# A batch of two attentions on one core: the third item's denominators, the projection's additions and the last weight sums

## The chip, the cores and the metric

The kernel runs on one core of a Trainium2 chip. The metric is the time of one launch on the device, in microseconds; the median of several runs is given, and one more execution was recorded by the hardware profiler.

## The reference

For each of 16 images (256 channels, 32 x 32 = 1024 positions) two layers are computed, all in float32. The part that matters here is the second attention, with 8 heads of 32 channels:

```python
# layer 0: 4 heads of 64 channels
qkv = (xs @ w_proj + b_proj).reshape(B, S, N_HEADS, 3 * D_K)
attn = softmax(einsum('bihd,bjhd->bijh', q, k) * SCALE, axis=2)
x = einsum('bijh,bjhd->bihd', attn, v) @ w_out + b_out + xs
# layer 1: 8 heads of 32 channels, then an MLP
x = x + attention(group_norm(x, gn1_w, gn1_b), qkv_w, proj_w, proj_b, phys_bias)
h = group_norm(x, gn2_w, gn2_b)
return x + mlp_w2 @ gelu(mlp_w1 @ h + mlp_b1) + mlp_b2
```

## The kernel before

One image of the batch is called b here. For each b the kernel runs attention a (layer 0), attention b (layer 1) and the MLP, and it weaves the pieces of the neighbouring images into them: while attention b of image b runs, TensorE also makes the MLP's output for image b - 1 (tiles m, lines 1180 and on) and q, k, v of layer 0 for image b + 1 (tiles v_a). A stage is a Python generator; after each of its steps, functions that were put off with `later.after(steps, fn)` and have come due are run, and the pieces of other work for that step are issued. So the order of the instructions on an engine is mostly the order in which this Python runs.

Attention b (`attention_b`) works through four items: (t, c) with t one of two halves of 512 positions, and c one of two groups of four heads. An item takes eight blocks of 128 keys in four steps of two blocks. In a step, `scores` makes the scores s_b on TensorE (line 569) and their exp e_b on ScalarE (line 582), `weigh` multiplies the exps of the step before with v (acc_b, line 619), and `add` sums the exps over the key blocks on VectorE into the tile es_b (line 595), which becomes the softmax's denominator. Results of single steps are copied out by ScalarE (lines 630 and 634) and added by VectorE (line 603); the very last one of a stage is added from PSUM (line 637).

For images 1 to 14 (`by_fold`) the denominators of the first three items, i = 0 to 2, go through `fold`: two DMAs, one on SP's queue and an accumulating one on GpSimd's, pack the sums into a tile packed_b (lines 649 and 650). A few steps later `normalise_folded` makes the denominators with 16 small matmuls (den_b, line 659). The fourth item, i = 3, goes through `normalise`, with 8 matmuls from es_b itself (den_b, line 676). Both call `denominators`: ScalarE copies the row out of PSUM (line 376), a DMA on SP spreads it over the partitions (sp_b, line 381), VectorE takes the reciprocal (line 387), DMAs on SP write it to a row in DRAM (lines 391 or 398) and read it back onto all partitions (rd_b, line 403), and `scale` multiplies the item's result with it (line 701). GpSimd keeps two running totals (lines 399 and 400).

When both items of a half t are scaled, `out_proj` multiplies with the projection's weights (tiles j, line 357). For t = 0 of images 1 to 14 there is a spare place, the other half of the tile packed_b: ScalarE copies the product with its bias there (line 745), VectorE adds it to x (line 748) and takes statistics for the coming group norm (line 753). The projection of t = 1 is handed to attention a of the next image and is issued at that stage's thirteenth step.

PSUM has two single banks (0 and 1, `bank`) and three pairs (`wide`). acc_b uses bank 0, den_b bank 1. The exps stand in a ring of four tiles (`weights_tile`); an exp of attention b takes a whole tile per key block, one of attention a half a tile. `tc.keep_in_program_order(ins)` holds an instruction where it was issued; `with tc.issue_after(ins)` puts what is issued in it behind ins on that engine.

Of the kernel before, what the change touches and what calls it, by code (L numbers as in the profile page):

```python
# [259 lines left out]
def first_pass(ctx, tc, x, out, k):  # L260
    nc = tc.nc
# [3 lines left out]
    later = Later()  # L265
# [44 lines left out]
    def wide(name, n=None):  # L310
        if n is None:
            n = next(m for m in order if m not in kept)
        use(n)
        return ps_s.tile([P, 2, TB], F32, tag=f"s{n}", name=name)

    def bank(name, n):
        return ps_a.tile([P, TB], F32, tag=f"b{n}", name=name)
# [36 lines left out]
    def product(o, w, r, **flags):  # L354
        for c0 in range(0, P, cols[0]):
            sl = slice(c0, c0 + cols[0])
            nc.tensor.matmul(o[sl], w[:, sl], r, **flags)  # L357
# [15 lines left out]
    spread_out, spare = {}, {}  # L373

    def denominators(key, den, d, full, waits, then, parts=1):
        nc.scalar.copy(d, den)
        n = full.shape[1]
        w = 4 * TB // P
        spread = work.tile([P, w], F32, tag="spread", name=f"sp_{key}", bufs=2)
        row = dram.tile([4 * TB // n, n], F32, tag="row", name=f"row_{key}", bufs=4)  # L380
        nc.sync.dma_start(
            spread, d[:: 32 // parts].rearrange("p (a b) -> p a b", b=w)
        )

        def invert():
            inverse = work.tile([P, w], F32, tag="inverse", name=f"inv_{key}", bufs=2)
            tc.keep_in_program_order(nc.vector.reciprocal(inverse, spread))
            if parts > 1:
                num = P // parts
                for r in range(parts):  # L390
                    nc.sync.dma_start(
                        row[:, r * n // parts : (r + 1) * n // parts].rearrange(
                            "g (a b) -> g a b", b=w
                        ),
                        inverse[r * num : (r + 1) * num],
                    )
            else:
                nc.sync.dma_start(row.rearrange("r (a b) -> (r a) b", b=w), inverse)
            nc.gpsimd.tensor_add(dsum, dsum, spread)  # L399
            nc.gpsimd.tensor_add(isum, isum, inverse)  # L400
            num = P * n // (4 * TB)
            for r in range(P // num):
                spread_out["last"] = nc.sync.dma_start(
                    full[r * num : (r + 1) * num], row[r].partition_broadcast(num)
                )
            later.after(waits[1], lambda: then(full))

        later.after(waits[0], invert)
# [133 lines left out]
    def attention_b(b, qT, kT, v, project):  # L542
        key, D = f"b_{b}", D1
        G = P // D


        by_fold = 0 < b < B - 1
# [3 lines left out]
        units = [(i, kb) for i in range(len(items)) for kb in range(0, SB, 2)]  # L551
# [36 lines left out]
        def add(i, kb, es):  # L588
            if kb == 0:
                sums[i] = work.tile([P, G, TB], F32, tag="es", name=f"es_{key}_{i}", bufs=2)  # L590
            step = G if by_fold else G // 2
            for m in range(kb == 0, 2):
                for g in range(0, G, step):
                    d = sums[i][:, g : g + step]
                    ins = nc.vector.tensor_add(  # L595
                        d, (d if kb else es[0][:, g : g + step]), es[m][:, g : g + step]
                    )
                    if by_fold or m or g:
                        tc.keep_in_program_order(ins)
                    yield  # L600
            while parts:
                r, part = parts.pop(0)
                tc.keep_in_program_order(nc.vector.tensor_add(r, r, part))
# [41 lines left out]
        def fold(i, r):  # L645
            if i == 0:
                packs.append(act.tile([P, 4, TB], F32, tag="res", name=f"packed_{key}"))
            packed = packs[0][:, i % 2 * 2 : i % 2 * 2 + 2]
            nc.sync.dma_start(packed, sums[i][:HALF])
            nc.gpsimd.dma_start(packed, sums[i][HALF:], accum_op=ALU.add)  # L650
            later.after(3 if i else 4, lambda: normalise_folded(i, r, packed))

        def normalise_folded(i, r, packed):
            c = items[i][1]
            q = TB // G
            den = bank(f"den_{key}_{i}", 1)[:, :q]
            for m in range(2):
                for n in range(G):
                    nc.tensor.matmul(
                        den[n * D : (n + 1) * D, :], k["folded"][:, c, m],  # L660
                        packed[:, m, n * q : (n + 1) * q], start=m == 0, stop=m == 1,
                    )
            if i == 1:
                spare["home"] = packs[0]
            full = work.tile([P, TB], F32, tag="full", name=f"rd_{key}_{i}", bufs=2)
            denominators(
                f"{key}_{i}", den, full[:, :q], full, (1, 2 if i < 2 else 4),
                lambda full: scale(i, r, False, full), G,
            )
# [29 lines left out]
        def scale(i, r, last, full):  # L699
            t, c = items[i]  # L700
            tc.keep_in_program_order(nc.vector.tensor_mul(r, r, full))
            if c == CC - 1:
                issue = project(t, res[t])
                if last and b + 1 < B:
                    handed.append(issue)
                else:
                    later.after(1, issue)
# [3 lines left out]
        for u in units:  # L711
            now = scores(*u)
            adds = add(*now)
            if pending:
                if not by_fold and now[1]:
                    next(adds)
                weigh(*pending)
            else:
                yield
            for _ in adds:  # L720
                pass
            if pending:
                yield
            pending = now
# [6 lines left out]
    def out_proj(key, w, src, bias, xs, t, stats, then):  # L731
        todo = list(range(CC))

        def issue(cos=range(CC), apart=False):
            home = None if apart else spare.pop("home", None)
            apart = apart or cols[0] == P
            if not apart:
                both = wide(f"{key}_{t}")
            ps = {}

            def leave(co):
                y = xs[:, co, t * TB : (t + 1) * TB]
                if home is not None:
                    held = home[:, 2 + co]
                    nc.scalar.activation(
                        held, ps[co], AF.Identity, bias=bias[:, co : co + 1]
                    )
                    nc.vector.tensor_add(y, y, held)
                else:
                    nc.vector.scalar_tensor_tensor(  # L750
                        y, ps[co], bias[:, co : co + 1], y, ALU.add, ALU.add
                    )
                nc.vector.bn_stats(stats[:, co, t, :], y)
                todo.remove(co)

            for co in cos:
                ps[co] = bank(f"{key}_{t}_{co}", co) if apart else both[:, co, :]
                for kc in range(CC):
                    product(
                        ps[co],  # L760
                        w[:, kc, co * P : (co + 1) * P],
                        src(kc),
                        start=(kc == 0),
                        stop=(kc == CC - 1),
                    )
                if apart:
                    leave(co)
            if not apart:
                for co in cos:
                    leave(co)  # L770
            if not todo and then:
                then()

        return issue
# [945 lines left out]
```

## Time and profile before

| | |
|---|---|
| median of 3 runs | 3627.85 us (3626.86 to 3628.85) |
| the profiled execution's own time | 3625.52 us |
| its span, from the first to the last instruction | 3623.4 us |
| TensorE clock granted, mean | 0.999 |
| VectorE: es_b, 128x2048 (line 595, adding to the sum) | 336 times, mean 2287 ns |
| VectorE: es_b, 128x1024 (line 595, images 0 and 15) | 96 times, mean 1218 ns |
| VectorE: x plus packed_b (line 748) | 28 times, mean 678 ns |
| VectorE: statistics (line 753) | 128 times, mean 687 ns |
| TensorE: den_b from packed_b (line 659) | 672 times in 42 groups of 16 |

The distance from the first line 748 of one image to that of the next is 223 to 224 us. Tile names are printed without their numbers, so den_b stands for the denominators of every image and item, and the line tells the kind. A group of matmuls that run side by side in parts of the array has a busy time that is shorter than the sum of its durations; where times within TensorE are compared, the start of one group is subtracted from the start of the next.

### The profile page before, as it was taken

The numbers are of one execution on the slowest core, as the hardware profiler recorded it, in microseconds if no ns is written. First come the engines' busy times: TensorE is split into PE (matmuls) and PEld (weight loads), VectorE is DVE, ScalarE is ACT, GpSimd is POOL, SyncE is SP. The second block draws the span as 40 slices with busy tenths as digits, with TensorE's granted clock in tenths as the row PEclk, the third lists the DMA queues.
The fourth block names the chain that finished last, engine by engine and source line by source line (L and its number), as shares of the span: only waits on it lengthen the run. The fifth ranks groups of instructions, "written<-read, shape, count | busy, mean of one in ns | idle before, by whom it ended". The sixth has DMA issues, their size and how long they took to land.

```text
span 3623.4 us, 81637 instructions
## 1 busy us (share of the span) xinstructions
PE 3590.2 (99%) x35565; PEld 1470.2 (41%) x35565; DVE 2775.8 (77%) x3153; ACT 2283.5 (63%) x3197; POOL 244.0 (7%) x317
## 2 busy tenths in 40 slices
PE   9999999999999999999999999999999999999998
PEld 3434344343443434434344443444434444343433
DVE  5586887768778687876868778688786977868887
ACT  4665757657575675756658566585765757657572
POOL 4000100001000010000100001010010100000000
PEclk9999999999999999999999999999999999999999
DMA  3011321213122131221312213121121212213100
GB/s 129 10 50 37 59 78 34 77 33 71 60 40 72 39 81 45 49 67 34 81 45 52 66 33 81 45 55 63 42 73 44 55 62 48 72 39 65 59 22 23
DMA packets 81571, 198.29 MB, mean 55 GB/s; under 512 B 37974, under 2 KB 38742, under 8 KB 75062
## 3 DMA queue, kind: packets, MB, share of 16 engines
q1 hardware_dynamic: 71828, 164.39, 14.9%
q0 software_dynamic: 7632, 28.21, 5.1%
q8 instruction: 280, 4.59, 0.5%
q10 hardware_dynamic: 1746, 0.40, 0.1%
q14 instruction: 85, 0.70, 0.1%
HBM read 125.85 MB, written 22.27 MB: 41 GB/s over the span
## 4 chain that ended last, share of the span: by engine, by line
PE 77%; DVE 12%; issue 4%; DMA 4%; SPq 2%; ACT 1%; DVEq 0%; ACTq 0%; POOL 0%; POOLq 0%
PE s_a L428 12%; PE acc_a L451 12%; PE m L1097 10%; PE s_b L569 8%; PE m L357 7%; DVE es_b L595 7%; PE acc_b L619 7%; PE qk_b L1003 3%; PE qk_a L1003 3%; PE v_b L357 3%; PE o L357 3%; PE j L357 2%; DMA rd_b<-row_b 2%; PE qk7y_b L1003 1%; PE qk7y_a L1003 1%
## 5 line engine op out<-in xcount | busy, mean ns | idle before, releaser
L582 ACT ACTIVATE e_b<-s_b 128x1024 f32<-128x1024 f32 (+1 forms) x1280 | 982.1, 865 | 137.0 <-PE s_b L569 137.0
L595 DVE TENSOR_TENSOR es_b<-es_b,e_b 128x2048 f32<-128x2048 f32 (+1 forms) x432 | 880.6, 2049 | 103.8 <-ACT e_b L582 86.0
L438 ACT ACTIVATE e_a<-s_a 128x1024 f32<-128x1024 f32 x512 | 520.6, 1024 | 360.4 <-PE s_a L428 356.2
L428 PE MATMUL s_a<-q,k 64*64 64x512 f32 x4096 | 544.4, 593 | 0.0
L451 PE MATMUL acc_a<-e_a,v 64*64 64x512 f32 x4096 | 540.3, 589 | 0.0
L569 PE MATMUL s_b<-q,k 32*64 32x512 f32 x8192 | 527.4, 600 | 4.0 <-DVE res_b L637 2.0
L465 DVE TENSOR_TENSOR es_a<-es_a,e_a 128x1024 f32<-128x1024 f32 x384 | 473.5, 1233 | 59.5 <-ACT e_a L438 36.2
L619 PE MATMUL acc_b<-e_b,v 128*32 128x512 f32 x4096 | 492.1, 598 | 0.0
L357 PE MATMUL m<-g,w 128*32 128x256 f32 (+1 forms) x6456 | 416.6, 385 | 0.0
L357 PEld LDWEIGHTS m<-g,w 128*32 128x32 f32 x6456 | 223.9, 111 | 204.3 <-issue 58.9
L451 PEld LDWEIGHTS acc_a<-e_a,v 64*64 64x64 f32 x4096 | 188.2, 133 | 251.3 <-issue 214.9
L569 PEld LDWEIGHTS s_b<-q,k 32*64 32x64 f32 x8192 | 175.8, 130 | 257.5 <-issue 132.6
L428 PEld LDWEIGHTS s_a<-q,k 64*64 64x64 f32 x4096 | 176.1, 133 | 246.5 <-issue 209.1
L619 PEld LDWEIGHTS acc_b<-e_b,v 128*32 128x32 f32 x4096 | 108.5, 109 | 351.6 <-ACT e_b L582 194.7
L1097 PE MATMUL m<-gn_h,w 128*128 128x512 f32 x512 | 242.5, 602 | 2.9 <-DVE x L1222 1.3
L595 DVE TENSOR_TENSOR es_b<-e_b,e_b 128x2048 f32<-128x2048 f32 (+1 forms) x72 | 147.0, 2050 | 127.6 <-ACT e_b L582 127.6
L1161 DVE TENSOR_TENSOR g<-g,g 128x512 f32<-128x512 f32 (+1 forms) x185 | 195.5, 1068 | 1.2 <-PE m L357 0.8
L1097 PE MATMUL m<-hs,w 128*128 128x512 f32 x384 | 177.9, 592 | 0.1
L1112 ACT ACTIVATE g<-g,m1b 128x512 f32<-128x512 f32 x128 | 91.5, 720 | 110.9 <-DVE g L1141 83.4
L1097 PEld LDWEIGHTS m<-gn_h,w 128*128 128x128 f32 x512 | 93.1, 190 | 118.8 <-issue 101.1
L1112 ACT ACTIVATE g<-m,m1b 128x512 f32<-128x512 f32 x128 | 80.9, 683 | 76.7 <-PE m L1097 76.7
L399 POOL TENSOR_TENSOR dsum<-dsum,sp_b 128x16 f32<-128x16 f32 x63 | 72.9, 1157 | 795.8 <-DMA sp_b<-rd_b 795.8
(214 smaller groups left out, 3591.9 us busy)
## 6 DMA issues: line engine op xcount, KB each, us to landing
w<-w_kept SPq DMA_DIRECT2D x30, 1792.0 KB
packed_b<-es_b SPq DMA_DIRECT2D x42, 512.0 KB
packed_b<-es_b POOLq DMA_DIRECT2D x42, 512.0 KB, 6.2
d_a<-row_a SPq DMA_DIRECT2D x64, 256.0 KB
rd_b<-row_b SPq DMA_DIRECT2D x252, 64.0 KB
out_dram<-x SPq DMA_DIRECT2D x63, 256.0 KB
x<-in_x_dram SPq DMA_DIRECT2D x30, 512.0 KB
qk<-qk_kept SPq DMA_DIRECT2D x14, 1024.0 KB
```

Of the source, the lines that this page charges most:

```text
L357: nc.tensor.matmul(o[sl], w[:, sl], r, **flags)
L428: nc.tensor.matmul(s[h : h + HALF, g, :], kT[g * D : (g + 1) * D, c, kb * P + h : kb * P + h + HALF], qT[g * D : (g + 1) * D, c, t * TB : ...
L438: nc.scalar.activation(e, s, AF.Exp, scale=float(D) ** -0.5)
L451: nc.tensor.matmul(accs[i][h][g * D : (g + 1) * D, :], v[h * HALF : (h + 1) * HALF, kb, c * 2 + g], e[h * HALF : (h + 1) * HALF, g, :], st ...
L465: nc.vector.tensor_add(sums[i], held[i] if kb == 1 else sums[i], e)
L569: nc.tensor.matmul(outs[g][h : h + HALF, :], kT[g * D : (g + 1) * D, c, k0 : k0 + HALF], qT[g * D : (g + 1) * D, c, t * TB : (t + 1) * TB] ...
L582: nc.scalar.activation(to, s, AF.Exp, scale=float(D) ** -0.5)
L595: ins = nc.vector.tensor_add(d, (d if kb else es[0][:, g : g + step]), es[m][:, g : g + step])
L619: nc.tensor.matmul(acc[g * D : (g + 1) * D, :], v[:, kb + m, c * G + g], es[m][:, g, :], start=(m == 0), stop=(m == 1),)
L1003: nc.tensor.matmul(to, w, x[right], start=first, stop=True, skip_group_check=not first)
L1097: nc.tensor.matmul(ps, blocks[1][number - 1][:, i * P : (i + 1) * P], inputs[b][number], start=first, stop=True, skip_group_check=not first,)
L1161: (nc.vector.tensor_add if plus else nc.vector.tensor_sub)(d, d, more)
```

## The change

There are four edits. The denominators of the third item (i = 2) are made four steps after its fold instead of three. In the last step of the fourth item the weight sums are taken in halves of 1024 columns instead of whole tiles of 2048. The additions of the projection of t = 0 to x and their statistics are put off by one step, and they are placed behind the last weight sum on VectorE. To have that place, every weight sum of attention b is remembered in `spread_out["es"]`.

```diff
@@ -588,13 +588,15 @@
         def add(i, kb, es):
             if kb == 0:
                 sums[i] = work.tile([P, G, TB], F32, tag="es", name=f"es_{key}_{i}", bufs=2)
-            step = G if by_fold else G // 2
+            step = G if by_fold and (i, kb) != units[-1] else G // 2
             for m in range(kb == 0, 2):
                 for g in range(0, G, step):
                     d = sums[i][:, g : g + step]
                     ins = nc.vector.tensor_add(
                         d, (d if kb else es[0][:, g : g + step]), es[m][:, g : g + step]
                     )
+                    spread_out["es"] = ins
+                    spread_out["es"] = ins
                     if by_fold or m or g:
                         tc.keep_in_program_order(ins)
                     yield
@@ -648,7 +650,7 @@
-            later.after(3 if i else 4, lambda: normalise_folded(i, r, packed))
+            later.after(3 if i == 1 else 4, lambda: normalise_folded(i, r, packed))
@@ -745,13 +747,19 @@
                     nc.scalar.activation(
                         held, ps[co], AF.Identity, bias=bias[:, co : co + 1]
                     )
-                    nc.vector.tensor_add(y, y, held)
+                    later.after(1, lambda: add_up(co, y, held))
+                    return
                 else:
                     nc.vector.scalar_tensor_tensor(
                         y, ps[co], bias[:, co : co + 1], y, ALU.add, ALU.add
                     )
                 nc.vector.bn_stats(stats[:, co, t, :], y)
                 todo.remove(co)
+
+            def add_up(co, y, held):
+                with tc.issue_after(spread_out["es"].ins):
+                    nc.vector.tensor_add(y, y, held)
+                    nc.vector.bn_stats(stats[:, co, t, :], y)
```

The two programs have the same instructions on every engine except VectorE, which has 28 more (two per image 1 to 14). At the end of attention b of each of these images VectorE's order becomes: four sums of 1024 columns, the addition to x, line 603's addition, the statistics, the second addition and its statistics, line 637's addition, the third item's reciprocal, the fourth item's reciprocal, two sums of attention a (line 465), and then the scaling of the third item (line 701). Before, it was: two additions to x, two statistics, two sums of 2048 columns, line 603, the third reciprocal, line 637, the scaling of the third item, the fourth reciprocal, and then the sums of attention a. On TensorE the 16 matmuls of the third item's denominators move from ahead of the projection j to behind the acc_b of the following step, ahead of a v_a; on ScalarE their copy moves accordingly. On SP the fourth item's spread (line 381) moves ahead of the four reads (line 403) of the third item's rows.

## The prediction

> **What bounds the kernel now.** I read the page first (who is busy, the chain that ended last), then the waits, then the order of time at the one place that the change touches, on TensorE and on VectorE. The page and its chain:
>
> ```profile
> span 3623.4 us, 81637 instructions
> PE 3590.2 (99%) x35565; PEld 1470.2 (41%) x35565; DVE 2775.8 (77%) x3153; ACT 2283.5 (63%) x3197; POOL 244.0 (7%) x317
> PE 77%; DVE 12%; issue 4%; DMA 4%; SPq 2%; ACT 1%; DVEq 0%; ACTq 0%; POOL 0%; POOLq 0%
> ```
>
> TensorE is busy 99% of the span, so work moved on VectorE counts only where TensorE waits for it. The edit acts in items 1 to 14 of the batch, at the end of the second attention. In the table of waits the largest VectorE wait there is not TensorE's:
>
> ```profile
> DVE room_b L701 <- DMA rd_b<-row_b: 96.6, 15, 7.7
> ```
>
> That is VectorE idle for 6.4 us per item before the third item's scaling (L701), behind which the next attention's sums stand. The order of time of TensorE, for item 4, shows that TensorE runs on through it (start, length, what; in brackets the idle time before it):
>
> ```profile
> 1096.05 0.62 PE L659 MATMUL den_b<-packed_b,folded 128*32 128x128 f32 x16
> 1096.49 3.62 PE L357 MATMUL j<-res_b,wpj 128*32 128x512 f32 x32
> 1100.04 2.54 PE L569 MATMUL s_b<-q,k 32*64 32x512 f32 x32
> 1102.51 1.92 PE L619 MATMUL acc_b<-e_b,v 128*32 128x512 f32 x16
> 1104.25 1.91 PE L357 MATMUL v_a<-wp,x 128*32 128x256 f32 x32
> 1105.98 1.90 PE L619 MATMUL acc_b<-e_b,v 128*32 128x512 f32 x16
> 1107.69 1.91 PE L357 MATMUL v_a<-wp,x 128*32 128x256 f32 x32
> 1110.13 1.07 PE L676 MATMUL den_b<-es_b,eones 128*32 128x512 f32 x8 [0.53 <-DVE es_b L595]
> ```
>
> The only gap is at the fourth item's denominators (L676), which need the last weight sums. By start times it is longer: the last v_a takes 1110.13 - 1107.69 = 2.44 us until the next start, the one before it 1.73, so 0.71 us are lost. VectorE's order shows why the sums are late:
>
> ```profile
> 1096.58 0.69 DVE L701 TENSOR_TENSOR res_b<-res_b,rd_b 128x512 f32<-128x512 f32 x1 [1.81 <-DMA rd_b<-row_b]
> 1097.18 0.68 DVE L1226 TENSOR_TENSOR x<-x,packed_b 128x512 f32<-128x512 f32 x1
> 1097.79 4.68 DVE L595 TENSOR_TENSOR es_b<-es_b,e_b 128x2048 f32<-128x2048 f32 x2
> 1102.38 0.71 DVE L603 TENSOR_TENSOR room_b<-room_b 128x512 f32<-128x512 f32 x1
> 1103.02 1.28 DVE L748 TENSOR_TENSOR x<-x,packed_b 128x512 f32<-128x512 f32 x2
> 1104.22 1.27 DVE L753 BATCH_NORM_STATS2 st<-x 128x6 f32<-128x512 f32 x2
> 1105.42 4.66 DVE L595 TENSOR_TENSOR es_b<-es_b,e_b 128x2048 f32<-128x2048 f32 x2
> 1109.99 0.69 DVE L603 TENSOR_TENSOR room_b<-room_b 128x512 f32<-128x512 f32 x1
> ```
>
> From L701 on VectorE does not idle until the last sum ends near 1110.06. L701 itself (second item's scaling) waits for a DMA, and the projection j needs its result too. So both engines start from one event, the end of L701 at 1097.27, and race to L676: VectorE gets there after 1110.13 - 1097.27 = 12.86 us, TensorE would be earlier.
>
> **What the Trainium skill says.** "VectorE: DVE Perf Modes", section "Side-by-side: where the cycles go for N=2048 bf16", counts one result a cycle in the 1x mode plus some 158 cycles at 0.96 GHz; I estimate 2298 ns for 2048 columns and 1231 for 1024. The trace agrees: the two forms of L595 have means of 2287 and 1218 ns. "PSUM — Partial Sum Buffer", section "Engine vs sequencer instructions", calls the queues of ScalarE and VectorE strict FIFO and TensorE's matmuls in program order; so an instruction is late with whatever stands ahead of it, as the chain above shows. "DMA: Bandwidth & Descriptors", section "Latency and other measured facts", gives a DMA about 2 us of fixed cost; here the small transfer of a denominator (L381, issued at 1098.35) ended GpSimd's wait at 1100.34, 2.0 us.
>
> **The change part by part.** Times are relative to the first L748 of an item (1103.02 in item 4), read from the order of time of all fourteen items; L701 of the second item ends at -5.75 in each.
>
> *Denominators a step later.* The 16 matmuls of L659 go from ahead of j to behind the acc_b that starts at 1102.51, ahead of a v_a. From start to start they take 0.43 or 0.44 us in all 42 groups of the trace, 28 of them between an acc_b and 256-column matmuls as in the new place: I take 0.44, bounds 0.4 and 0.7. In front of j nothing is won unless L701 was not the limit. The later part of j cannot start before -5.69 (item 1: 427.95, its L748 at 433.64). In nine items (1, 4, 5, 8, 9, 10, 13, and 3 and 7 within 0.05) j already ends at -2.98 to -2.93, set by L701; in 2, 6, 12 it is 0.04 to 0.09 later, in 11 and 14 it is 0.46 and 0.53 later. Afterwards all end at about -2.98. The waits of L659 for its packing DMA (0.15 to 1.01 us before j in items 3, 6, 7, 8, 9, 12) go, but j then waits for L701 instead.
>
> *Additions behind the last sums.* Two L748 and two L753 stood in front of the sums: 1105.42 - 1103.02 = 2.40 us. Moved behind, the sums start at 0.0 instead of 2.40. Nothing reads these columns of x before the group norm, which comes after the other half's j, 29 us later (462.58 in item 1). What is queued behind them is L637, which frees bank 0 for acc_a; see below.
>
> *1024 columns.* Four adds for two: 4 x 1.16 us from start to start (four in a row take 4.63 in the first item) against 4.66: nothing. Each half follows its own exp; the last exp ends at +2.13, before the fourth half starts at 3.48. The sums end at 4.7 instead of 7.06.
>
> *The sum for TensorE.* From j's end at -2.98: s_b 2.47 (part of it a wait for ScalarE's copy of j, L745, which stays), acc_b 1.74, L659 0.44, v_a 1.73, acc_b 1.72, v_a 1.73. L676 starts at +6.85, and what is late next is TensorE itself, the sums being there 2.1 us earlier. Before, L676 started at +7.12 in 13 items and +7.47 in item 12. Saved: 13 x 0.27 + 0.62 = 4.1 us. With L659 at its bounds of 0.4 and 0.7 the gain is 4.7 to 0.5.
>
> *The rest of VectorE.* After the sums: add, L603, statistics, add, statistics, L637, each 0.6 from start to start: L637 ends near 8.35, before 8.46; acc_a needs its bank at 10.7. The third reciprocal comes at 8.25 instead of 7.58, and its four row writes on SP follow. SP now issues the fourth item's spread (L381) ahead of the four reads of the third's rows, at about 11.1 instead of 13.4, so the fourth reciprocal runs at about 13.1; the third's L701 now stands behind it and two of the next sums (L465). VectorE still stands still, parked at that reciprocal from 8.5 to 13.1, but L465 starts near 13.3 instead of 15.96. The rows land about 0.7 + 0.6 later, at 16.4, when L701 comes up: little wait. L465 was not holding TensorE at 15.96 (no gaps in the next 10 us), so starting earlier is worth nothing. The loads of w and x behind these issues start about 1 us earlier, also worth nothing. ScalarE's copy of the denominators (0.34) moves with them into slack of 0.60 before a v copy. GpSimd keeps its order; its two small adds have no waiter.
>
> **Rivals.**
>
> A, the forecast: TensorE bounds the end of the stage, 4.1 us saved: 3625.52 - 4.1 = 3621.4 in the terms of the profiled execution. The median shown, 3627.85, is 2.3 above that execution; I add it: 3623.8.
>
> B, faster: the wait of s_b for the copy of j (2.47 against 1.91 from start to start elsewhere) goes as well, 14 x 0.56 = 7.8 more, 3616.0. For it: it is the one other loss on this stretch. Against: j's end, L745 and the order on ScalarE there are as before.
>
> C, the sums are no earlier, for a reason that I don't see, or the moved matmuls cost 0.7: TensorE arrives at 7.12 as before and L659 only fills the old wait: 0, 3627.8. For it: nothing but that VectorE is always the later one now. Against: no input of the halves comes after +2.13.
>
> D, slower: VectorE parks too long at the fourth reciprocal, with every sum of the next attention behind it. Its place is the ring of weight tiles: the ninth exp of attention a (at +21.3) needs the first tile back, so the first L465 must have ended by then. It decides once the fourth denominator's spread lands after about +20, against 13.1 worked out. From there each us costs 14: at +21, 3627.85 - 4.1 + 14 = 3637.8. For it: the spread now waits on SP behind four row writes, which wait for the third reciprocal, behind six moved instructions. Against: seven us of margin.
>
> **How the numbers follow.** About 0.2% (7.3 us) is what a measurement of this kernel can tell from no change. A has 0.75, B 0.09, C 0.09, D 0.07. A's own range, from L659's bounds and about 2 us of luck in the DMA waits ahead of L701 (items 1 and 8 lose 1 us there, others none), is 3621 to 3628. Of A, 0.03 passes 0.2% on the fast side; B nearly always does. That gives faster 0.11, same 0.82, slower 0.07. For 8 in 10 I take 3617.5 to 3629.5, into B and past C.
>
> **What would show it.** Right: no gap before the fourth item's denominators, which start 12.6 us after the second item's L701 ends instead of 12.86; a gap in j of about 0.4 us more where the denominators were; VectorE's long idle stretch ahead of a reciprocal instead of L701; L465 about 2.5 us earlier. Wrong: a gap left at L676, a start-to-start time of the moved matmuls above 0.5, a new gap at acc_a or at the exps of attention a.

## The result, and the profile after

The changed kernel takes 3622.53 us, the median of 19 runs (3619.73 to 3624.66), against 3627.85 us (3624.95 to 3631.59, also 19) for the kernel before. The ratio is 0.9986 with a 95% interval of 0.998 to 0.9992, that is 2.9 to 7.3 us less. The forecast was 3623.8.

The profiled execution took 3623.73 us. Its page begins, with the engines' share of the chain that ended last:

```profile
span 3621.7 us, 81706 instructions
PE 3588.2 (99%) x35565; PEld 1471.2 (41%) x35565; DVE 2781.4 (77%) x3181; ACT 2283.7 (63%) x3197; POOL 229.9 (6%) x317
PE 81%; DVE 8%; issue 4%; DMA 3%; SPq 2%; ACT 1%; DVEq 0%; ACTq 0%; POOL 0%
```

TensorE is still busy for 99% of the span. In the chain VectorE has fallen from 12% to 8%, and TensorE has risen from 77% to 81%: part of the chain that went through VectorE's sums (line 595, from 7% to 4%) now stays on TensorE. The order of time of TensorE in item 4 is the place where this is seen (start, length, what; in brackets the idle time before it):

```profile
1098.71 1.04 PE L357 MATMUL j<-res_b,wpj 128*32 128x512 f32 x8
1100.31 2.78 PE L357 MATMUL j<-res_b,wpj 128*32 128x512 f32 x24 [0.56 <-DVE res_b L703]
1103.02 2.54 PE L569 MATMUL s_b<-q,k 32*64 32x512 f32 x32
1105.49 1.92 PE L621 MATMUL acc_b<-e_b,v 128*32 128x512 f32 x16
1107.23 0.62 PE L661 MATMUL den_b<-packed_b,folded 128*32 128x128 f32 x16
1107.67 1.91 PE L357 MATMUL v_a<-wp,x 128*32 128x256 f32 x32
1109.40 1.90 PE L621 MATMUL acc_b<-e_b,v 128*32 128x512 f32 x16
1111.12 1.91 PE L357 MATMUL v_a<-wp,x 128*32 128x256 f32 x32
1112.84 1.04 PE L678 MATMUL den_b<-es_b,eones 128*32 128x512 f32 x8
```

The new lines move most numbers on: L703 was L701 (the scaling), L661 was L659 (the third item's denominators), L678 was L676 (the fourth's). The gap ahead of the fourth item's denominators is gone: the last v_a takes 1112.84 - 1111.12 = 1.72 us until the next start, where it took 2.44. But a gap has appeared inside j. With the denominators no longer ahead of it, it starts 1.54 us before the scaling's end (0.78 in the kernel before), and then stops until the scaling is done. VectorE's order in the same item:

```profile
1099.56 0.69 DVE L703 TENSOR_TENSOR res_b<-res_b,rd_b 128x512 f32<-128x512 f32 x1 [2.14 <-DMA rd_b<-row_b]
...
1105.97 4.62 DVE L595 TENSOR_TENSOR es_b<-es_b,e_b 128x1024 f32<-128x1024 f32 x4
1110.51 0.68 DVE L761 TENSOR_TENSOR x<-x,packed_b 128x512 f32<-128x512 f32 x1
...
1114.23 0.25 DVE L387 RECIPROCAL inv_b<-sp_b 128x16 f32<-128x16 f32 x1
1119.14 0.25 DVE L387 RECIPROCAL inv_b<-sp_b 128x16 f32<-128x16 f32 x1 [4.67 <-issue]
1119.31 1.16 DVE L465 TENSOR_TENSOR es_a<-e_a 128x1024 f32<-128x1024 f32 x1
...
1122.90 0.69 DVE L703 TENSOR_TENSOR room_b<-room_b,rd_b 128x512 f32<-128x512 f32 x1 [1.09 <-DMA rd_b<-row_b]
```

The second item's scaling ends at 1100.25. The last sums end at 1110.59, so 10.34 us later, and TensorE asks for them at 1112.84, 12.59 us later: VectorE has 2.3 us to spare where before it was the late one. The idle time of VectorE now stands ahead of the fourth item's reciprocal, and the next attention's first sum (L465) starts 19.06 us after the scaling instead of 21.70. In the table of waits (engine, what waits, for what: us in total, times, longest) the change of place is seen over all items:

```profile
DVE inv_b L387 <- DMA sp_b<-rd_b: 33.3, 8, 4.7
DVE inv_b L387 <- issue: 32.6, 7, 4.9
```

These two rows hold 65.9 us that VectorE spent in front of L387; the 96.6 us in front of the third item's scaling have shrunk to 3.4. TensorE's own rows moved as well. In the kernel before they were

```profile
PE den_b L676 <- DVE es_b L595: 6.4, 12, 0.8
PE j L357 <- DVE res_b L701: 1.6, 2, 0.8
```

and in the changed one the first has gone, while j's waits for the scaling grew:

```profile
PE j L357 <- DVE res_b L703: 8.3, 12, 1.6
```

In all 14 items L678 starts 12.59 us after the scaling's end (before: 12.85 to 12.87 in 13 items and 13.21 in item 12). From the scaling of item 1 to that of item 14 the kernel before took 3331.5 - 427.9 = 2903.6 us and the changed one 3330.1 - 430.7 = 2899.4, so 4.2 us less. That stretch holds the stage's end of thirteen items (the fourteenth lies behind it). The earlier starts of L678 in these are worth 3.9 us, and each group of the fourth denominators itself takes 0.97 us to the next start instead of 1.00, another 0.4 us: together 4.3. The spans of the two profiled executions differ by only 1.7 us, because the changed one was already 2.6 us later at its first scores, ahead of any changed instruction. In the order of time of TensorE in the kernel before, and then after, these scores are

```profile
32.67 1.95 PE L428 MATMUL s_a<-q,k 64*64 64x512 f32 x16
```

```profile
35.29 1.09 PE L428 MATMUL s_a<-q,k 64*64 64x512 f32 x8
```

This is the reason to compare stretches between two events of the changed stage, and not whole spans, when the sum is about 4 us.

### The profile page after: what moved, and what is told of

The parts are those of the page before. It is cut to its first block, busy times and chain, and to the rows that moved or that the text cites. A ratio compares the mean times of both kernels' runs of the same rounds, so it can differ in the third digit from the quotient of the medians.

```text
span 3621.7 us, 81706 instructions
## 1 busy us (share of the span) xinstructions
PE 3588.2 (99%) x35565; PEld 1471.2 (41%) x35565; DVE 2781.4 (77%) x3181; ACT 2283.7 (63%) x3197; POOL 229.9 (6%) x317
## 4 chain that ended last, share of the span: by engine, by line
PE 81%; DVE 8%; issue 4%; DMA 3%; SPq 2%; ACT 1%; DVEq 0%; ACTq 0%; POOL 0%
PE s_a L428 12%; PE acc_a L451 12%; PE m L1105 10%; PE s_b L569 8%; PE acc_b L621 8%; PE m L357 7%; DVE es_b L595 4%; PE qk_b L1011 3%; PE qk_a L1011 3%; PE v_b L357 3%; PE o L357 3%; PE j L357 3%; PE v_a L357 2%; DMA rd_b<-row_b 2%; PE qk7y_b L1011 1%
## 5 line engine op out<-in xcount | busy, mean ns | idle before, releaser
L438 ACT ACTIVATE e_a<-s_a 128x1024 f32<-128x1024 f32 x512 | 520.8, 1024 | 360.2 <-PE s_a L428 357.4
L465 DVE TENSOR_TENSOR es_a<-es_a,e_a 128x1024 f32<-128x1024 f32 x384 | 474.1, 1235 | 69.2 <-ACT e_a L438 49.7
L357 PE MATMUL v_a<-wp,x 128*32 128x256 f32 (+1 forms) x1856 | 121.5, 379 | 0.0
```

The source lines that it names most:

```text
L438: nc.scalar.activation(e, s, AF.Exp, scale=float(D) ** -0.5)
L465: nc.vector.tensor_add(sums[i], held[i] if kb == 1 else sums[i], e)
```

## Experiments

The theory: two engines race from the end of the second item's scaling to the fourth item's denominators. The time that an engine needs from the one to the other is called its arm here. Moving the additions makes VectorE the earlier one; moving the denominators does nothing by itself but put 0.44 us onto TensorE's arm; the halves do nothing. The main rival: the denominators' wait for their packing DMA is what the gain comes from. The first four experiments share 43 runs of the kernel before, with a median of 3627.75 us.

**The denominators alone.** Only the third item's denominators come a step later.

```diff
-            later.after(3 if i else 4, lambda: normalise_folded(i, r, packed))
+            later.after(3 if i == 1 else 4, lambda: normalise_folded(i, r, packed))
```

> The third item's denominators a step later, alone. Theory (two engines race from the end of the second item's scaling to the fourth item's denominators, and VectorE comes last at 12.86 us): VectorE's arm is as before, so L676 still starts at 12.86, only its gap shrinks from 0.53 to about 0.1 us; time as before, 3627.8 (3626 to 3629). Rival (what the change gains is the wait for the packing DMA ahead of the projection): about 4 us less, 3623.5.

Measured: 3628.06 us in 13 runs, ratio 1.0 (0.9992 to 1.0009). The rival's gain is not there. Order of time of item 4, the scaling on VectorE (it ends at 1098.27), then TensorE:

```profile
1097.58 0.69 DVE L701 TENSOR_TENSOR res_b<-res_b,rd_b 128x512 f32<-128x512 f32 x1 [2.08 <-DMA rd_b<-row_b]
...
1105.25 0.62 PE L659 MATMUL den_b<-packed_b,folded 128*32 128x128 f32 x16
...
1109.13 1.91 PE L357 MATMUL v_a<-wp,x 128*32 128x256 f32 x32
1111.21 1.06 PE L676 MATMUL den_b<-es_b,eones 128*32 128x512 f32 x8 [0.17 <-DVE es_b L595]
```

L676 starts 1111.21 - 1098.27 = 12.94 us after the scaling, no earlier than before, and still waits for VectorE. The gap shrank from 0.53 to 0.17 because the denominators now fill a part of it. A gap that gets smaller is no gain when the instruction behind it starts at the same time.

**The additions alone.** The denominators stay ahead of j, the sums stay whole; the additions and statistics go behind the last sum.

```diff
+                    spread_out["es"] = ins
@@
-                    nc.vector.tensor_add(y, y, held)
+                    later.after(1, lambda: add_up(co, y, held))
+                    return
```

(with add_up as in the change.)

> The additions to x behind the last weight sums, alone: sums of 2048 columns, the third item's denominators where they were before. Theory: VectorE's arm shortens to about 10.5 us, TensorE's arm has no 0.44 us of L659 in it, so L676 starts at 12.15 us after the scaling in most items (12.2 to 12.6 where the projection was not held by the scaling); about 9 us less than before, 3618.8 (3617 to 3621), better than the change. Rival (the three edits need each other): no better than the change, 3622.5 or more.

Measured: 3617.25 us in 7 runs (3615.84 to 3618.03), ratio 0.9971 (0.996 to 0.9982). By the medians one part of the change gives twice the gain of the whole (10.5 us against 5.3), and each of these 7 runs is below each of the 19 of the whole change. Order of time of item 4, the scaling on VectorE (it ends at 1097.15), then TensorE:

```profile
1096.46 0.69 DVE L702 TENSOR_TENSOR res_b<-res_b,rd_b 128x512 f32<-128x512 f32 x1 [1.95 <-DMA rd_b<-row_b]
...
1095.83 0.65 PE L660 MATMUL den_b<-packed_b,folded 128*32 128x128 f32 x16
1096.26 3.73 PE L357 MATMUL j<-res_b,wpj 128*32 128x512 f32 x32
1099.92 2.54 PE L569 MATMUL s_b<-q,k 32*64 32x512 f32 x32
1102.40 1.92 PE L620 MATMUL acc_b<-e_b,v 128*32 128x512 f32 x16
...
1107.58 1.91 PE L357 MATMUL v_a<-wp,x 128*32 128x256 f32 x32
1109.31 1.04 PE L677 MATMUL den_b<-es_b,eones 128*32 128x512 f32 x8
```

L677 starts 12.15 us after the scaling in nine items, and 12.17 to 12.82 in the other five; nowhere is there a gap. In the nine the difference to the whole change is 12.59 - 12.15 = 0.44 us, the denominators' start-to-start time. Ahead of j they cost nothing there, because j cannot run through until the scaling is done: they stand in a wait. Behind it they are paid in full. In the five items TensorE came to j too late to be held by the scaling, so there the denominators cost time ahead of j too.

**The change without the halves.** The denominators later and the additions behind, with the sums in 2048 columns.

```diff
-            step = G if by_fold and (i, kb) != units[-1] else G // 2
+            step = G if by_fold else G // 2
```

> The change without its halves: denominators a step later and additions moved, the last sums in 2048 columns. Theory: the halves give nothing, since the sums are ready about 2 us before TensorE asks for them; L676 at 12.6 us, time as the change, 3622.5 (3621 to 3624.5). Rival (the halves are what brings the sums forward): L676 later than 12.6, time between 3624.5 and 3628.

Measured: 3623.81 us in 13 runs, ratio 0.9989 (0.9981 to 0.9997), against 0.9986 (0.998 to 0.9992) for the whole change. Order of time of item 4, VectorE (the scaling ends at 1098.29), then TensorE:

```profile
1104.39 4.69 DVE L595 TENSOR_TENSOR es_b<-es_b,e_b 128x2048 f32<-128x2048 f32 x2 [0.29 <-ACT e_b L582]
...
1110.88 1.04 PE L677 MATMUL den_b<-es_b,eones 128*32 128x512 f32 x8
```

The fourth denominators start 12.59 us after the scaling in all 14 items, as in the change. The halves do bring the sums forward: with whole tiles VectorE waits 0.29 us for an exp, and the sums end 10.78 us after the scaling instead of 10.34. But VectorE is not the late engine any more, so the time does not show it. This run differs from the additions alone by the denominators' place only: 12.59 against 12.15 us in most items, and 3623.81 against 3617.25 us.

**The projection j a step later.** After the additions alone, TensorE's arm still holds two losses: j's wait for the scaling, and the scores behind j, which take 2.47 us from start to start instead of 1.91. Would a later j remove them? Its rival: the waits only move. The edit is to the additions alone, in `scale`:

```diff
-                    later.after(1, issue)
+                    later.after(2 if by_fold else 1, issue)
```

> The additions moved, and the projection of t = 0 issued a step later, behind the next scores and acc_b, so that TensorE has 3.6 us of other work between the scaling's due time and the projection. Theory: TensorE no longer waits for the scaling (its wait was up to 1.1 us) nor for the copy of the projection in the next scores (0.56 us); L676 10.5 to 12.2 us after the scaling; about 19 us less than before, 3609 (3606 to 3613). Rival (the wait only moves: the copy of the projection then holds its PSUM pair against v_a or the next attention): no better than the additions alone, 3618 or more.

Measured: 3622.39 us in 21 runs, ratio 0.9987 (0.9981 to 0.9994): some 5 us worse than the additions alone, and the expectation missed. L677 starts 11.94 to 13.23 us after the scaling. Order of time of TensorE, item 4:

```profile
1096.12 0.64 PE L660 MATMUL den_b<-packed_b,folded 128*32 128x128 f32 x16
1096.69 3.09 PE L569 MATMUL s_b<-q,k 32*64 32x512 f32 x32
1099.70 1.92 PE L620 MATMUL acc_b<-e_b,v 128*32 128x512 f32 x16
1101.45 3.62 PE L357 MATMUL j<-res_b,wpj 128*32 128x512 f32 x32
```

j runs without a wait, but the scores, which had j's 3.66 us ahead of them, now come directly after the denominators and take 1099.70 - 1096.69 = 3.01 us. The table of waits has, on the queue of weight loads (PEld), before and in this run:

```profile
PEld s_b L569 <- ACT room_b L634: 23.2, 56, 0.4
PEld s_b L569 <- ACT room_b L635: 35.7, 70, 1.1
```

The 14 extra waits, as many as the items, hold 12.5 us or 0.9 us each; the scores lose 1.10 us in item 4. The waits are for ScalarE's copy of acc_b out of PSUM bank 0 (L635), a bank that the next scores take too. In item 4 this copy stands behind the exps and ends at 1097.60. Two of the scores' weight loads go ahead of it, the third waits 0.77 us and comes 0.05 us after its end. Order of time of ScalarE, then of the weight loads:

```profile
1096.97 0.63 ACT L635 COPY room_b<-acc_b 128x512 f32<-128x512 f32 x1
```

```profile
1096.69 0.19 PEld L569 LDWEIGHTS s_b<-q,k 32*64 32x64 f32 x2 [0.20 <-issue]
1097.65 0.62 PEld L569 LDWEIGHTS s_b<-q,k 32*64 32x64 f32 x18 [0.77 <-ACT room_b L635]
```

So the rival's number (3618 or more) came true, but the wait is another than the one it named (the copy of j).

**The projection exchanged with a piece of v_a.** If the scores only need 1.9 us of any work ahead of them, another piece can give it. In the table of the pieces that fill the steps, j's old place gets the piece of v_a that stood one step behind:

```diff
-                [], first[2:3],
+                first[2:3], [],
```

(on top of the previous edit.)

> The additions moved as in the run with them alone, and the projection of t = 0 changes places with the first of the two late pieces of v_a, so that every pair of scores still has other work ahead of it and the projection comes 5.4 us later. Theory (TensorE's stall is the projection's wait for the scaling, and what spoiled the run with the projection a step later was scores without other work ahead of them, which wait for ScalarE's copies out of banks 0 and 1): the scores take 1.91 us again, no wait at the projection, none at L676; 17 to 20 us less than before, 3609 (3606 to 3612). Rival (ScalarE or VectorE is next to be late at this place whatever the order): 3616 or more, not better than the additions alone.

Measured: 3605.44 us in 5 runs (3604.79 to 3606.14), against 3626.14 in 9 runs of the kernel before; ratio 0.9941 (0.9927 to 0.9955). This is 20.7 us less, and 0.6 us below the expected range. Order of time of TensorE, item 4:

```profile
1092.07 1.92 PE L357 MATMUL v_a<-wp,x 128*32 128x256 f32 x32
1093.93 1.97 PE L569 MATMUL s_b<-q,k 32*64 32x512 f32 x32
1095.83 1.92 PE L620 MATMUL acc_b<-e_b,v 128*32 128x512 f32 x16
1097.57 3.62 PE L357 MATMUL j<-res_b,wpj 128*32 128x512 f32 x32
1101.00 1.90 PE L620 MATMUL acc_b<-e_b,v 128*32 128x512 f32 x16
```

The scores take 1.90 us and j 3.43 (to the next start at 1101.00). With the additions alone they took 2.48 and 3.66, so 0.58 + 0.23 = 0.81 us are won in item 4. The v_a ahead of the scores takes 1.86 us instead of 1.73, so 0.68 remain, or 9.5 in 14 items; the medians, each against its own runs of before, give 20.7 - 10.5 = 10.2. TensorE has no wait left for the scaling here; what is left are waits of the third item's denominators for their packing DMA:

```profile
PE den_b L660 <- DMA packed_b<-es_b: 3.6, 5, 1.0
```

**The exchange, with the denominators later.** The first experiment's line on top of that. With j no longer behind a wait, the denominators cost the same in either place, and a step later their DMA has landed.

> As the run with the projection and a piece of v_a exchanged, with the third item's denominators a step later as well, now ahead of the projection in its new place. Theory: in front of the projection L659 costs its 0.44 us there instead of in the earlier place, so nothing by itself, and the waits for its packing DMA (2.5 to 4 us in all fourteen) go: 3606 (3602 to 3610), faster than without it. Rival (the packing wait only makes room for other waits): same as without it, within 1.5 us.

Measured: 3603.11 us in 5 runs (3601.36 to 3604.29), ratio 0.9933 (0.9919 to 0.9946) against the same runs of before. The intervals of the two versions overlap, but every run of this one is below every run of the other, and the packing wait fell to

```profile
PE den_b L660 <- DMA packed_b<-es_b: 0.4, 1, 0.4
```

So the same edit that did nothing alone, and cost 6.6 us beside the moved additions, is worth about 2 us here. This is the best version seen, 23.0 us (0.6%) below the kernel before by the medians. Item 3 shows the next limit. Order of time of VectorE, then of TensorE:

```profile
873.50 0.69 DVE L702 TENSOR_TENSOR res_b<-res_b,rd_b 128x512 f32<-128x512 f32 x1 [3.21 <-DMA rd_b<-row_b]
...
879.91 4.68 DVE L595 TENSOR_TENSOR es_b<-es_b,e_b 128x2048 f32<-128x2048 f32 x2
```

```profile
882.65 1.91 PE L357 MATMUL v_a<-wp,x 128*32 128x256 f32 x32
884.74 1.06 PE L677 MATMUL den_b<-es_b,eones 128*32 128x512 f32 x8 [0.18 <-DVE es_b L595]
```

Here TensorE's arm has become the shorter one, and the sums are late again, 884.74 - 874.19 = 10.55 us after the scaling: VectorE's new arm, seen directly. Its sums, in whole tiles, end 10.40 us after the scaling and not 10.78, because no sum waits for an exp: the scores now stand ahead of j. The two arms are not wholly independent.

## Why the prediction was right

- **The race and its new winner.** TensorE's arm was put at 12.60 us from the scaling's end (6.85 + 5.75); it measured 12.59 in all 14 items. VectorE's sums were put at 4.7 + 5.75 = 10.45 us and end at 10.34; TensorE comes later, so the start of L678 does not show them. In item 3 of the last experiment, where VectorE is the late one, L677 starts at 10.55. The gap in j was to grow by about 0.4 us per item: its row of waits grew from 1.6 to 8.3 us, 0.48 per item.
- **The denominators.** 0.44 us was taken, with bounds of 0.4 and 0.7. They take 0.44 from start to start in all 14 items in the new place, and 0.44 is the difference between the whole change and the additions alone in nine items. The step said that in front of j nothing is won unless the scaling was not the limit: j ends 2.77 us after the scaling in all 14 items of the change, and did so, within 0.01 us, in seven before. The denominators alone can't show this by their ratio of 1.0, since VectorE is the late engine there.
- **The additions.** That moving them carries the gain is shown by the additions alone. What I did not draw from my own sum: without the denominators TensorE's arm is 12.60 - 0.44 = 12.16, and the saving up to 0.7 us per item instead of 0.27. The text priced both edits and did not say that one takes back most of the other.
- **The halves.** Priced at nothing, because four sums of 1024 columns take as long as two of 2048. That they start without the wait for a whole tile's exps, and so end 0.44 us earlier, was not in the sum. For the time it makes no difference: the change without them gives the same 12.59.
- **The rest of VectorE.** L465 was put at 19.05 us after the scaling (13.3 + 5.75) and is at 19.06; the fourth reciprocal at 18.85, and is at 18.89. These are item 4; over the 14 items L465 is at 18.95 to 19.31. The third item's scaling was put at 22.15 with little wait; it starts at 21.39 to 22.65, and item 4, shown above, has the longest wait, 1.09 us. TensorE did not feel it: from L678 to the next projection it takes 21.73 us in every item.
- **The size.** 4.1 us were forecast for fourteen items. Between the same two events in both traces, with thirteen ends of the stage, it is 4.2, of which the sum of the prediction gives 3.9. The medians differ by 5.3, with 2.9 to 7.3 in the interval: the forecast is inside, and the runs can't tell the remaining 1.2 from nothing.
- **The rivals.** B (the scores' wait for the copy of j goes too) did not happen: the scores still take 2.47 us. Its price, 7.8 us, was about right: the exchange of j and v_a removed that wait, and 0.58 of the 0.81 us in item 4 are this. C (the sums no earlier) falls with the changed kernel's own order: they end 10.34 us after the scaling. D needed the fourth spread to land after +20; it landed near +13, and nothing was late behind it. Its threshold was not tried.

## What to carry to other kernels

When two engines race to one instruction, work out the arrival of each from the event that both start from, and judge every edit by the arm it is on: taking time from the late arm gains only down to the other arm, and a part of the same change can lengthen that one. An instruction that stands inside another wait is free there, so moving it out of the wait costs its full time (0.44 us per item here). Change the parts one at a time before keeping them together. And before moving a long piece away from in front of something, ask what that piece was covering, and put another in its place.

## What was not expected of the hardware

- A TensorE that shows 99% busy and hardly a gap still loses time inside its groups. The same 32 matmuls of s_b took 1.91, 2.47 and 3.01 us from start to start in different places, all without an idle time ahead of them in the order of time of item 4. What the last one waits for shows in the table of waits of the weight loads (12.5 us more in 14 more waits), and hardly in TensorE's own (1.6 us in 7). That table alone is no measure either: the best version has 14 more waits in the same row (29.0 us in 70, none over 0.4), and its scores take 1.91 us, because a v_a runs ahead of them. The distance between starts is the measure.
- The recorded idle time also understates the loss: ahead of the fourth denominators 0.53 us were recorded in item 4, while the starts show 0.71.
